# A four-layer hybrid network whose work is woven together by charged costs: other charges for TensorE's products

## The chip, the core and the metric

The kernel runs on one core of a Trainium2 chip. The core has five engines that take their instructions in program order and meet through semaphores: TensorE (PE, matrix products, with PEld for its weight loads), VectorE (DVE), ScalarE (ACT), GpSimd (POOL) and SyncE (SP, which here issues nearly all transfers). The metric is the device time of one execution in microseconds: the median of three runs was 6643.48 us (6634.54 to 6644.86).

## What is computed

An image batch of 4 x 32 x 32 positions with 256 channels runs through four layers. In the reference, cut to what matters here:

```python
# layer 0: selective scan over 1024 positions, 512 channels, 64 states
def step(h, inp):
    xt, dtt, Bt, Ct = inp
    dA = jnp.exp(dtt[:, :, None] * A)
    h = dA * h + (dtt * xt)[:, :, None] * Bt[:, None, :]
    y = jnp.einsum('bdn,bn->bd', h, Ct)
    return (h, y)
...
x = _L0_conv_ref(x, ...)       # norm, product, 3x3 convolution, scan, product
x = _L1_conv_ref(x, ...)       # 1x1, grouped 3x3, 1x1 convolutions
t = t + _L2_attn_ref(_ln_t(t), ...)   # attention of 8 heads over 1024 positions, masked by edges
t = t + _L2_ffn_ref(_ln_t(t), ...)    # 8 experts of 256, best two weighted
t = t + _L3_attn_ref(_ln_t(t), ...)   # products, a scan with 16 states, product
t = t + _L3_ffn_ref(_ln_t(t), ...)    # 8 experts of 512, best two weighted
```

Every expert is computed for every position, and the weights of those not chosen are zero.

## The kernel before

**Two streams of work.** The first is the scans (`scans`, L356). There are eight, one for each of the four images in layer 0 (written (0, b)) and in layer 3 (written (3, b)); `SCANS` (L31) sets their order: (0,0), (0,1), (3,0), (0,2), (3,1), (0,3), (3,2), (3,3). A scan of layer 0 has 256 units of 128 rows x 1024 positions, one of layer 3 has 64, so that there are 1280 units in all. One unit is: a transfer of `dA` (L430), an exponential on ACT (`decay`), two bf16 products on TensorE that spread the inputs into `ps_rep` (`first`, L445), a product and the scan itself on VectorE (`TENSOR_TENSOR` and `TENSOR_TENSOR_SCAN`), and a product on POOL. For every two units, four f32 products with 32 output rows each (`pair`, L460) collect the result in the four quarters of `ps_y`.

The second stream is all other work, in stages (`STAGES`, L33), written as generators. `front` b (norm, convolution and the scan's inputs of layer 0), `middle` b (the end of layer 0, layer 1, attention, the experts of layer 2, and `front3`, which makes the inputs of scan (3, b)) and `last` b (the end of layer 3's scan and its experts). Stage `middle` b can begin when scan (0, b) is done, or, if nothing else can, when its first half is; `last` b likewise after (3, b). `advance` (L530) takes the first stage in the list that can begin and does one step of it.

**How they are woven.** `Metered` (L92) passes each engine call on and adds a charge in microseconds to that engine's clock; the charge of a TensorE product is `matmul_us`. `run` (L552) goes through the scans; twice in every unit it does up to two steps of the current stage, but none as soon as the clock of any engine is ahead of VectorE's:

```python
for e in clock:
    clock[e] = max(clock[e], now - LAG)
for _ in range(TICKS):
    if max(clock.values()) > clock["vector"] + LEAD or self.advance() is None:
        break
```

So the charges fix the order in which instructions stand in each engine's queue, and nothing else. They are worked out when the program is built; they delay nothing at run time.

**When inputs are late.** A scan's inputs are asked for 12 units ahead (`AHEAD`). If the stage that makes them isn't that far, the request is put off until 5 units before they are used (`LATEST`); then `need` (L517) does all steps of the stage that are still missing, one after the other, before the next unit is written. In the text this is a stop of the scans. Inside one, attention (`heads`, L1320) puts its scores into the scan's own PSUM tiles (`ps_sx` in place of `ps_sc`). After the last unit, whatever stages remain are done in a row: the tail.

**Names.** In attention, a key block is one step of `heads`: two score products (`qT`, `kT`, 32 contraction rows), two shifts (`mT`, bf16, 32 rows), two masks (`maskT`, bf16) and four value products with 32 output rows (`ps_at`). In the experts (`moe`, L1442) `ps_h` is the first product (128 x 512 out), `ps_e` the second (128 x 256 out), and `tb` the sum on VectorE. In `front3` (L1624) `ps_p` are the inputs, `ps_g` the gates, `ps_c` the middle product, `ps_x` the small one and `ps_dt` the step sizes. Line 124 of the profile is that of the metered call, and so the line of nearly every instruction.

Of the kernel before, what the change touches and what calls it, by code (L numbers as in the profile page):

```python
# [8 lines left out]
BF16 = mybir.dt.bfloat16  # L9
# [54 lines left out]
def columns(x):  # L64
    n = 1
    for k in x.shape[1:]:
        n *= k
    return n


def matmul_us(out, lhsT=None, rhs=None, **_):
    if lhsT is None:
        lhsT = out
    us = 0.46e-3 * columns(out)
    if lhsT.dtype != BF16:
        us = max(4 * us, 0.3)
    if out.shape[0] <= 32:
        return us / 4
    return us / 2 if lhsT.shape[0] <= 32 else us


def by_columns(per, fixed, of=0):
# [9 lines left out]
class Metered:  # L92


    COST = {
        "tensor": {"matmul": matmul_us, "transpose": lambda out, *_: 0.3},
        "vector": {
            "tensor_tensor": by_columns(1.18, 0.06), "scalar_tensor_tensor": by_columns(1.5, 0.06),
# [1749 lines left out]
```

## Time and profile before

| | us |
|---|---|
| median of 3 runs | 6643.48 |
| the profiled execution | 6636.95 |
| its span, first to last instruction | 6635.2 |
| PE busy | 5360.8 |
| DVE busy | 5224.0 |
| POOL busy | 3653.8 |
| ACT busy, 497 + 96 loads of its table (1.283 each) included | 3439.4 |
| the scans on DVE (1280 of 2.284) | 2924.0 |
| the products before them on DVE (1280 of 1.213) | 1552.8 |

The slices of the page's second part are 165.9 us each. A digit is the busy share in tenths; the row PEclk is the clock granted to TensorE. An f32 product leaves two records in the trace, a bf16 product one, and records of products that overlap are united in a group's busy time, so that its "mean of one" can be much more than its share of the busy time: the 4096 records of `ps_y` in layer 0's scans have a mean of 767 ns and 808.4 us of busy time.

### The profile page before, as it was taken

How to read it: one execution, taken by the hardware profiler on the slowest of the kernel's cores; microseconds unless marked ns; L12 is line 12 of the kernel's file. 1: busy time of each engine (PE TensorE's matmuls, PEld its weight loads, DVE VectorE, ACT ScalarE, POOL GpSimd, SP SyncE). 2: the span in 40 equal slices, each digit the busy share in tenths (PEclk: the TensorE clock that was granted, in tenths of full speed). 3: DMA queues.
4: the chain of work that ended last, by engine and by line, in shares of the span. 5: the costliest groups of instructions: out<-in, count | busy, mean ns of one | idle time of the engine just before them, and what ended most of it. 6: DMA issues, size and time to landing. Idle time of an engine off the chain costs nothing. (4 is left out here: it accounts for less than half of the span.)

```text
span 6635.2 us, 60077 instructions
## 1 busy us (share of the span) xinstructions
PE 5360.8 (81%) x20320; PEld 2159.1 (33%) x20320; DVE 5224.0 (79%) x4489; ACT 3439.4 (52%) x4114; POOL 3653.8 (55%) x1801
## 2 busy tenths in 40 slices
PE   6568778679798577979789779898699679878979
PEld 3003213122253022234235332243245222524656
DVE  8788998988798997789889997798999972248411
ACT  3426666445477334557658544477478344245411
POOL 0876786755557765555766665556856651045200
PEclk8558779589799568979879789989699789887989
DMA  2444554643245566335555664344644750146221
GB/s 74 151 153 157 182 171 163 190 139 124 101 153 170 190 168 155 112 116 172 175 165 168 189 166 133 105 139 169 200 154 161 196 148 21 45 131 169 74 64 35
DMA packets 348112, 936.90 MB, mean 141 GB/s; under 512 B 37140, under 2 KB 119648, under 8 KB 346144
## 3 DMA queue, kind: packets, MB, share of 16 engines
q1 hardware_dynamic: 345616, 930.35, 44.9%
q8 instruction: 172, 2.82, 0.2%
q0 software_dynamic: 2128, 2.13, 0.2%
q14 instruction: 196, 1.61, 0.1%
HBM read 842.59 MB, written 93.95 MB: 141 GB/s over the span
## 5 line engine op out<-in xcount | busy, mean ns | idle before, releaser
L124 POOL TENSOR_TENSOR h<-h,rows 128x1024 f32<-128x1024 f32 x1280 | 3033.0, 2372 | 1900.9 <-DVE h L124 1698.8
L124 DVE TENSOR_TENSOR_SCAN h<-dA,ps_rep 128x1024 f32<-128x1024 f32 x1280 | 2924.0, 2284 | 164.9 <-issue 25.2
L124 DVE TENSOR_TENSOR ps_rep<-ps_rep,rows 128x1024 f32<-128x1024 f32 x1280 | 1552.8, 1213 | 247.7 <-PE ps_rep L124 247.4
L124 ACT ACTIVATE dA<-dA,A_L_conv_A_log 128x1024 f32<-128x1024 f32 x1024 | 1148.6, 1145 | 609.6 <-DMA dA<-dt 528.6
L124 PE MATMUL ps_rep<-S,spread_L_conv_A_log 96*128 96x512 bf16 x2048 | 767.5, 465 | 702.5 <-DVE h L124 674.3
L124 PE MATMUL ps_y<-h,collect_L_conv_A_log 128*32 128x512 f32 x4096 | 808.4, 767 | 77.5 <-POOL h L124 76.5
L124 PE MATMUL ps_h<-xTm,we 128*128 128x512 f32 x1536 | 718.9, 608 | 1.4 <-DVE tb L124 1.4
L124 PE MATMUL ps_e<-we,h_m 128*128 128x256 f32 x3072 | 699.6, 381 | 2.3 <-ACT h_m L124 2.3
L124 ACT ACT_TABLE_LOAD x497 | 637.7, 1283 | 74.7 <-PE ps_h L124 41.7
L124 PEld LDWEIGHTS <-spread_L_conv_A_log 96*128 96x128 bf16 x2048 | 161.4, 103 | 1485.8 <-DVE h L124 1174.6
L124 PEld LDWEIGHTS ps_e<-we,h_m 128*128 128x128 f32 x3072 | 580.8, 190 | 146.8 <-issue 47.2
L124 DVE SCALAR_TENSOR_TENSOR tb<-ps_e,cw,tb 128x256 f32<-128x256 f32 x512 | 220.8, 474 | 411.1 <-PE ps_e L124 410.8
L124 ACT ACTIVATE h_m<-ps_h,cols 128x512 f32<-128x512 f32 x384 | 260.5, 687 | 485.9 <-PE ps_h L124 483.1
L124 ACT ACTIVATE p<-ps_sc 128x512 f32<-128x512 f32 x432 | 234.4, 594 | 474.7 <-PE ps_sc L124 464.8
L124 PEld LDWEIGHTS ps_h<-xTm,we 128*128 128x128 f32 x1536 | 292.9, 194 | 338.5 <-issue 294.0
L124 ACT ACTIVATE dA<-dA,A_L_attn_A_log 128x1024 f32<-128x1024 f32 x256 | 290.2, 1146 | 189.5 <-DMA dA<-dt 166.0
L124 PE MATMUL ps_at<-p,v 128*32 128x512 f32 x1024 | 354.8, 610 | 39.1 <-ACT p L124 28.2
L124 PE MATMUL ps_rep<-S,spread_L_attn_A_log 96*128 96x512 bf16 x512 | 184.9, 449 | 174.2 <-DVE h L124 163.3
L124 PE MATMUL ps_sc<-qT,kT 32*128 32x512 f32 x864 | 251.3, 653 | 30.1 <-issue 30.1
L124 PE MATMUL ps_at<-p,ones 128*32 128x512 f32 x1024 | 271.9, 610 | 0.0
L124 PEld LDWEIGHTS ps_y<-h,collect_L_conv_A_log 128*32 128x32 f32 x4096 | 107.6, 120 | 474.7 <-POOL h L124 226.9
L124 PE MATMUL ps_cv<-pad,diag 128*128 128x512 f32 x576 | 260.4, 594 | 0.0
(313 smaller groups left out, 5027.7 us busy)
## 6 DMA issues: line engine op xcount, KB each, us to landing
dA<-dt SPq DMA_DIRECT2D x1280, 512.0 KB
we<-in_L_ffn_W_dram SPq DMA_DIRECT2D x64, 512.0 KB
parts<-parts SPq DMA_DIRECT2D x64, 384.0 KB
S<-parts SPq DMA_DIRECT2D x96, 256.0 KB
dt<-sp_r SPq DMA_DIRECT2D x64, 256.0 KB
y<-yo SPq DMA_DIRECT2D x128, 128.0 KB
y_back<-y SPq DMA_DIRECT2D x64, 256.0 KB
we<-in_L_ffn_w_dram SPq DMA_DIRECT2D x64, 256.0 KB
```

Of the source, the lines that this page charges most:

```text
L124: return got(*args, **kw)
```

## The change

`matmul_us` gets other charges. No product, no transfer and no wait is added or removed by hand; the order in which the stages' steps stand between the scan units follows from the charges.

```diff
 def matmul_us(out, lhsT=None, rhs=None, **_):
     if lhsT is None:
         lhsT = out
-    us = 0.46e-3 * columns(out)
-    if lhsT.dtype != BF16:
-        us = max(4 * us, 0.3)
-    if out.shape[0] <= 32:
-        return us / 4
-    return us / 2 if lhsT.shape[0] <= 32 else us
+    n = columns(out)
+    few = lhsT.shape[0] <= 32
+    if lhsT.dtype == BF16:
+        return (0.45e-3 if few else 0.72e-3) * n
+    if out.shape[0] <= 32 and n > 32:
+        return 0.86e-3 * n
+    return max(0.09 + (1.1e-3 if few else 1.25e-3) * n, 0.4)
```

| product (output columns) | charge before, us | after |
|---|---|---|
| `ps_rep`, masks: bf16 (512) | 0.236 | 0.369 |
| shifts: bf16, 32 contraction rows (512) | 0.118 | 0.230 |
| `ps_y`, `ps_at`: f32, 32 output rows (512) | 0.236 | 0.440 |
| scores: f32, 32 contraction rows (512) | 0.471 | 0.653 |
| full f32 (512) | 0.942 | 0.730 |
| full f32 (256) | 0.471 | 0.410 |

Transposes keep their charge of 0.3.

## Prediction

> **What bounds the kernel now.** I read the page first, then the busy time by stretch (cut where the stages change), the time line of the scan loop, and the chain of waits.
>
> ```profile
> span 6635.2 us, 60077 instructions
> PE 5360.8 (81%) x20320; PEld 2159.1 (33%) x20320; DVE 5224.0 (79%) x4489; ACT 3439.4 (52%) x4114; POOL 3653.8 (55%) x1801
> ...
> PE   6568778679798577979789779898699679878979
> ...
> DVE  8788998988798997789889997798999972248411
> PEclk8558779589799568979879789989699789887989
> ```
>
> Two loads of about equal size share the span: the scans (VectorE) and everything else (mostly TensorE). Near the end the DVE row drops twice: in slices 34 and 35 (2 2), and from slice 38 on (4 1 1). There TensorE works alone. Everywhere else the scan loop sets the pace:
>
> ```profile
> 299.99 2.29 DVE L124 TENSOR_TENSOR_SCAN h<-dA,ps_rep 128x1024 f32<-128x1024 f32 x1
> 302.20 1.21 DVE L124 TENSOR_TENSOR ps_rep<-ps_rep,rows 128x1024 f32<-128x1024 f32 x1
> 303.53 2.29 DVE L124 TENSOR_TENSOR_SCAN h<-dA,ps_rep 128x1024 f32<-128x1024 f32 x1
> ```
>
> From scan start to scan start an undisturbed unit takes 3.54 to 3.55 us. There are 1280 units; the first scan starts at 204.4, the last at 6194.5. The next rows are stretches: busy time by engine, then granted clock, DMA share and GB/s. They are middle 0, last 0, the stop of the scans at unit 1211, and the tail after the last scan.
>
> ```profile
> 1248.90:2195.90 947.00, 777.76 (x3217) 289.10 (x3217) 806.97 (x660) 518.69 (x634) 558.95 (x268) 0.86 0.43 144
> 3306.20:3739.50 433.30, 387.62 (x1540) 198.03 (x1540) 402.99 (x327) 298.04 (x290) 264.86 (x119) 0.89 0.51 167
> 5494.20:5906.40 412.20, 358.59 (x1391) 165.50 (x1388) 75.76 (x183) 150.87 (x212) 44.58 (x35) 0.92 0.12 38
> 6196.80:6635.20 438.40, 392.77 (x1370) 263.74 (x1368) 60.31 (x154) 79.15 (x119) 17.14 (x13) 0.92 0.14 45
> ```
>
> In the first two the scans run and VectorE is the fuller engine; in the last two VectorE has 76 of 412 and 60 of 438 us. So: **work done beside the scans costs little, work left for a stop or the tail costs its full TensorE time.** I split the 5990.1 us from first to last scan: 1279 steps at 3.55 = 4540; the stop beyond its own step, 412.2 - 3.6 = 409; other VectorE work between the scans, 624 (every such instruction in program order times its group's mean); the remainder, 417, are stalls. By the same split in stretches of 16 units the stalls are 63 in the start and the fronts, 101, 92 and 96 in middles 0 to 2, 8 in each of last 0 and last 1, and 49 after that.
>
> **What the change charges, against what the trace shows.** Per unit the planner charges VectorE 3.55 us, and TensorE two `ps_rep` and two `ps_y` products: 4 x 0.2355 = 0.94 before; 2 x 0.369 + 2 x 0.440 = 1.62 after. What is left for other work is 2.61 before, 1.93 after. In the trace two `ps_rep` take 0.60 and the four `ps_y` of two units 1.06 together, so 1.13 a unit at the most:
>
> ```profile
> 2999.83 0.60 PE L124 MATMUL ps_rep<-S,spread_L_conv_A_log 96*128 96x512 bf16 x2
> ...
> 3000.36 1.06 PE L124 MATMUL ps_y<-h,collect_L_conv_A_log 128*32 128x512 f32 x8
> ```
>
> (x8 is four products: an f32 product leaves two records.) The mean of one `ps_y` record is 767 ns, but four lie beside each other; the new 0.44 charges them 1.76 for 1.06.
>
> One key block of attention (2 scores, 2 shifts, 2 masks, 4 value products) is charged 0.942 + 0.236 + 0.471 + 0.942 = 2.59 before and 1.306 + 0.461 + 0.737 + 1.760 = 4.26 after. In the stop at 5494, without scans, one block follows the other at 2.81 us (5506.79 to 5509.60). Two full products of an expert are charged 1.88 before, 1.46 after, and took 1.72 (four in 3.43, in the chain of work).
>
> So per unit the planner lets in: **attention** 2.61 / 2.59 = 1.0 block before, 1.93 / 4.26 = 0.45 after; a middle has 64 blocks, so 64 units become about 142. **Experts** 2.61 / 1.88 = 1.39 pairs before, 1.93 / 1.46 = 1.32 after: the shorter full products nearly cancel the dearer scan.
>
> The instruction orders of both programs, counted by scan unit (PE's `ps_rep` pairs), show just this. Before to after: front 3 ends at unit 254, 263. Middle 0 ends at 456; after, it isn't ready at 507, where the scan that needs it stops, and ends at 518. Middle 1 ends at 708, 802; last 0 at 814, 915; middle 2 at 1028; after, it isn't ready at 1147 (second stop). Last 1 lies at 1028 to 1134 before; after, it begins at 1222, where last 2 was. Middle 3 begins at 1134, 1158, and both stop at 1211. Behind the last scan lie the end of last 2 and last 3 before, and the end of last 1, last 2 and last 3 after. VectorE's queue is in order: at a stop every later scan step stands behind the stage's own VectorE steps.
>
> **The sum**, against the profiled execution (6636.95 us, span 6635.2).
> - One more last stage in the tail. Last 3 alone runs from the output DMA of last 2 (6328.99) to 6635.2: **+306**. It needs the full TensorE time, and nothing hides it.
> - The stop at 1211 starts with 53 units of middle 3 behind it, not 77: 52 us more attention and other products by these durations, at the rate of the stop: **+53**.
> - The stop at 507: the rest of front3, 8 gate halves, 8 conv, 2 low, 6 dt. In the trace the same run from the first gate product (5817.1) to the next scan (5906.4) takes 89 us; less its own step, **+86**.
> - The stop at 1147: the same with 16 transposes and 8 input halves (14.5 us for the latter in the chain of work, 3.5 for the former at 0.22 each): 107, **+104**.
> - VectorE work that leaves the scan loop: tail 69 to 119 us, stops 83 to 105: **-71**.
> - Stalls, 417 now. Attention proper has 36, 39 and 40 in middles 0 to 2, where TensorE's content is 3.8 to 4.1 us a unit, above the 3.55. After, it is 2.1 to 2.3. The nearest rows are the fronts' convolutions, 3.2 to 3.3 a unit with stalls of 0 per 16 units; I take 1.5 per 16, so 16 a middle: -67. Front3 and last 1 leave the loop: -20. The chains of normalization and routing stay, but lie wider apart: -20. **-107**, with 0 and -417 as ends.
>
> Sum: 306 + 53 + 86 + 104 - 71 - 107 = **+371**. ACT's table loads fall, by the instruction orders, from 597 to 442 (155 x 1.283 = 199 us): worth nothing, ACT is at 52%. With last 1 its loads leave SP's queue and come behind the scans, and at the two new stops the `parts` and `S` transfers and POOL's softplus steps stand ahead of the next scan step: they are inside the 89 us. Between stops ACT waits 694.6 us for `dA` loads and POOL 1698.8 for the scans, both ahead of no one: VectorE's own wait for `ps_rep` is 247.4 in all. Medians stand 6.5 above the profiled execution: 6643.5 + 371 = **7015 us**.
>
> **A rule against it: the clock.** The granted clock is 0.92 in the stop, 0.86 in middle 0, 0.71 in the fronts (TensorE 74% busy). After, attention leaves TensorE emptier. The fronts say that this costs nothing: the clock drops only as far as the load leaves room. The Trainium skill ("TensorE: Matmul & The Clock Gate", part 1) says that an idle window of some 3.4 us puts the array back to half clock. Had attention run at half clock throughout, 2.2 us a unit would take 4.4, and some 480 units would cost 0.85 each: an estimate of 400 us more. No run here shows that yet; the fronts' rows speak against it, and I take the rows.
>
> **Rivals.**
> 1. *Relief is larger* (0.14): stalls fall to about 100, and the two new stops cost only their products (69 + 86, less 7). 371 - 210 - 42 = +119, 6762; this case reaches 6700 to 6870. For it: experts at 3.5 to 3.9 a unit show stalls near 0. Against: the chains between the stages stall at low load too (18 us in the 16 units at 352).
> 2. *No relief* (0.10): stalls stay at 417, now at the restarts. +478, 7122 and up to 7220. For it: after each stop VectorE waits for SP's loads of `S` and `dA`. Against: the units after 1211 show few such stalls.
> 3. *Faster* (0.03): saturation of TensorE during attention was the real price, and thinning it frees more than the tail costs. It decides when the scan step outside stops falls from (5990 - 409) / 1279 = 4.36 us to below 3.93, since 549 us of new stops and tail have to be paid. Its whole store is 417 + 71 = 488; only with the tail and stops at bare products (253 for 306, 148 for 190) does it give 454 - 488 = -34, 6609.
> 4. *Nothing changes* is out: the charges rule the order, and the orders differ from the first fronts on.
>
> **Chances and range.** Forecast 0.73 (6870 to 7110: stalls between 165 and 405), rivals 0.14, 0.10, 0.03. The range 6860 to 7120 leaves out most of rivals 1 to 3. Faster by over 0.2% (13 us, about what a measurement can tell) 0.03, within 0.01, slower 0.96.
>
> **What would show it.** Three long gaps between scan starts, about 89, 107 and 465 us, at units 507, 1147 and 1211, where there is one of 412 now. A tail of some 745 us behind the last scan, with DVE at 1 or 2 tenths. Mean step outside stops about 4.22. PE's clock in attention near 0.7. The busy sums of DVE, PE and POOL unchanged, ACT some 200 less. I am wrong if the step outside stops falls below 4.0, if a stop at 507 costs over 150, or if the tail isn't one last stage longer.

## The result, and the profile after

The changed kernel takes 6921.95 us (median of 4 runs, 6916.13 to 6931.93), the one before 6640.8 beside it: a ratio of 1.0428, 95% interval 1.0414 to 1.0441. It is slower by 281 us; 371 were forecast, and the time lies in the forecast's own range. Of the page of the profile after, the lines that answer to those shown of before:

```profile
span 6914.4 us, 59861 instructions
...
PE 5438.6 (79%) x20320; PEld 2137.0 (31%) x20320; DVE 5221.3 (76%) x4489; ACT 3230.7 (47%) x3943; POOL 3649.0 (53%) x1801
...
PE   6558768778869777787868977886977988697979
...
DVE  8889999989989598998998998998949221861111
PEclk8558769778869888887978987887978889698989
```

The work is the same: as many products, DVE 5221.3 us for 5224.0, POOL 3649.0 for 3653.8; ACT has 209 us less, 199 of them table loads (442 for 597). What changed is where it lies. Up to slice 30 the row DVE is a little fuller than before, but for slices 14 and 30, where the new stops lie; and it ends in four slices with 1 for two. The stretches that answer to the stop and the tail of before (two new stops, the stop at unit 1211, the time behind the last scan):

```profile
2278.80:2359.90 81.10, 73.57 (x173) 29.44 (x171) 9.63 (x11) 39.20 (x58) 23.15 (x18) 0.98 0.19 66
5019.50:5121.80 102.30, 94.69 (x227) 39.36 (x227) 9.65 (x12) 52.25 (x78) 23.17 (x18) 0.96 0.19 62
5406.40:5867.40 461.00, 411.82 (x1668) 178.14 (x1664) 77.91 (x183) 165.47 (x228) 43.21 (x34) 0.92 0.10 30
6164.00:6914.40 750.40, 664.31 (x2310) 448.01 (x2310) 104.84 (x270) 135.21 (x204) 31.94 (x25) 0.91 0.16 48
```

In all four TensorE is 89 to 93% busy and VectorE 9 to 17%. The first one, seen on VectorE's time line:

```profile
2278.81 2.29 DVE L125 TENSOR_TENSOR_SCAN h<-dA,ps_rep 128x1024 f32<-128x1024 f32 x1 
2332.95 0.69 DVE L125 SCALAR_TENSOR_TENSOR sp_e<-ps_dt,sp_e 128x512 f32<-128x512 f32 x1 [51.85 <-ACT sp_l L125]
...
2358.68 1.22 DVE L125 TENSOR_TENSOR ps_rep<-ps_rep,rows 128x1024 f32<-128x1024 f32 x1 
2359.93 2.29 DVE L125 TENSOR_TENSOR_SCAN h<-dA,ps_rep 128x1024 f32<-128x1024 f32 x1 
```

The next scan step isn't slow, it stands behind front3's own steps (`sp_e`, `sp_x`), and these wait, through ACT, for front3's products:

```profile
2328.45 0.69 ACT L125 ACTIVATE sp_r<-ps_dt,cols 128x512 f32<-128x512 f32 x1 [2.95 <-PE ps_dt L125]
```

So 81 us pass from one scan start to the next. Against this, the scan loop between the stops got faster. Attention of middle 0, from its first to its last value product, before and after:

```profile
1465.70:1741.60 275.90, 264.58 (x1380) 70.06 (x1380) 213.79 (x135) 141.75 (x209) 145.66 (x65) 0.98 0.35 116
```

```profile
1487.60:1978.00 490.40, 399.59 (x1823) 84.82 (x1824) 462.31 (x283) 221.92 (x285) 317.85 (x139) 0.83 0.46 146
```

Before, 57 scan steps start in 275.9 us (4.84 us each), TensorE is 96% busy and VectorE 77%. After, 131 start in 490.4 us (3.74 each), TensorE is 81% busy and VectorE 94%. VectorE's wait for `ps_rep` fell from 247.4 us to 98.2 over the whole run:

```profile
DVE ps_rep L125 <- PE ps_rep L125: 98.2, 69, 8.4
```

The sum, by the split of the prediction, made alike for every kernel (steps of 3.55 us; scan gaps over 30 us are stops; products behind the last scan are the tail). Counted this way the kernel before has 413 us of stalls and 628 of other VectorE work. Stalls are the remainder, so an error in the other work shows in them with the opposite sign; these two columns are good to some 13 us.

| kernel | stops | tail | other VectorE work | stalls | span |
|---|---|---|---|---|---|
| before | 412 | 441 | 628 | 413 | 6635 |
| after | 81 + 102 + 461 | 753 | 557 | 228 | 6914 |

Stops +232 (each new one less its own step: +225), tail +312, VectorE work -71, stalls -185, first scan 2 earlier: +279, the difference of the spans.

### The profile page after: what moved, and what is told of

It reads as the page before. It is cut to its first block, busy times and chain, and to the rows that moved or that the text cites. A ratio compares the mean times of both kernels' runs of the same rounds, so it can differ in the third digit from the quotient of the medians.

```text
span 6914.4 us, 59861 instructions
## 1 busy us (share of the span) xinstructions
PE 5438.6 (79%) x20320; PEld 2137.0 (31%) x20320; DVE 5221.3 (76%) x4489; ACT 3230.7 (47%) x3943; POOL 3649.0 (53%) x1801
## 5 line engine op out<-in xcount | busy, mean ns | idle before, releaser
L125 DVE TENSOR_TENSOR ps_rep<-ps_rep,rows 128x1024 f32<-128x1024 f32 x1280 | 1549.7, 1211 | 98.7 <-PE ps_rep L125 98.2
L125 PE MATMUL ps_y<-h,collect_L_conv_A_log 128*32 128x512 f32 x4096 | 786.3, 761 | 79.0 <-POOL h L125 79.0
L125 ACT ACTIVATE p<-ps_sc 128x512 f32<-128x512 f32 x400 | 217.1, 594 | 778.9 <-PE ps_sc L125 778.8
L125 PE MATMUL ps_at<-p,v 128*32 128x512 f32 x1024 | 340.5, 704 | 12.2 <-ACT p L125 11.6
L125 PE MATMUL ps_at<-p,ones 128*32 128x512 f32 x1024 | 317.4, 703 | 0.0
L125 PE MATMUL ps_sc<-qT,kT 32*128 32x512 f32 x800 | 274.6, 761 | 29.9 <-issue 22.6
L125 POOL TENSOR_TENSOR sp_l<-sp_l,sp_e 128x512 f32<-128x512 f32 x64 | 81.0, 1266 | 387.2 <-DVE sp_e L125 351.6
```

The source lines that it names most:

```text
L125: return got(*args, **kw)
```

## The experiments

Each kernel was timed in three rounds beside the kernel before. The prediction's account is theory A; B says that each charge costs in proportion; C says that the dearer attention made the stages late, which is where the prediction laid the weight. Where a cut of `matmul_us` below has a minus line, it gives the old charge in the changed function's form. The split of all runs stands behind the last one.

**One charge at a time.** e1: only the narrow f32 products, the change's line `return 0.86e-3 * n`, all else as before.

```diff
     if out.shape[0] <= 32 and n > 32:
-        return 0.46e-3 * n
+        return 0.86e-3 * n
```

> Only the f32 products with 32 output rows get the new charge (0.44), all others the old one. Theory A (time = scan steps at 3.55 us + other VectorE work between them + stalls of a TensorE that is over-full in attention + work in stops and tail at TensorE's rate): by the instruction order middle 3 now begins when the last stop comes, so the stop at unit 1211 holds 590 us of products for 333 (+252), a small new stop at 507 (+30), tail +21, VectorE work out of the loop -66, stalls -170: about 6708 us (6660 to 6750). Theory B (time follows the total charge, each part in proportion; the whole change charges about 823 us more and cost 281): +733 charged, so +250: about 6890. A also expects one gap of about 660 us between scan starts at unit 1211 and a tail of about 460.

Measured: 6694.6 us, ratio 1.008 (1.0061 to 1.01). The total is A's and not B's, but by two misses of A that nearly cancel: the stop at 1211 takes 726 us for some 660, and the stalls fall by 243 for 170. The stop at 507 takes 34.

e2: only the other f32 products.

```diff
-    return max((0.92e-3 if few else 1.84e-3) * n, 0.3)
+    return max(0.09 + (1.1e-3 if few else 1.25e-3) * n, 0.4)
```

> Only the charges of the other f32 products change (full 0.73 for 0.94, scores 0.65 for 0.47), narrow and bf16 ones keep the old charge. Theory A: attention thins a little (0.885 key blocks a unit, 3.5 to 3.7 us of TensorE a unit), experts thicken to 4.3 to 4.8; stop at 1211 as before, tail -27, stalls -30 to -50: about 6575 us (6530 to 6640). Theory B: 377 us less charged, so -128: about 6513. A third theory, that the shorter full products are what cost the time because the experts over-fill TensorE, expects more than 6700.

Measured: 6788.65 us, ratio 1.0222 (1.0204 to 1.024). A missed by 214 us and B by more; the third theory is right. Stop (413) and tail (421) came about as said, but the stalls rose from 413 to 586. Counted per 16 units they show where. TensorE's content below is a unit's products at the rates of the stops and the tail of before, as an estimate: 0.86 us for a full f32 product of 512 columns, 0.43 for one of 256, 2.81 for a key block, and 0.86 for the scan's own as e11 charges them. In the 16-unit stretches of last 0 where most experts lie, the content is 4.1 to 4.3 us a unit in place of 3.5, with 3 to 7 us of stalls in place of none; the two last stages in the loop have 50 each for 8. The fronts (units 64 to 255), with up to 4.1 for 3.3, go from about 50 to about 100. Last 0's stretch in this kernel:

```profile
3338.30:3748.20 409.90, 371.54 (x1442) 197.56 (x1438) 350.56 (x292) 254.69 (x254) 224.87 (x102) 0.87 0.46 154
```

It has 89 units in 410 us, 4.6 us each; before it had 106 in 433, 4.1 each, with VectorE at 93% and not at 86%. Against the scans, last 0 is over sooner, and then, in 32 units before middle 2 may begin, no other work is there at all. In last 0's stretch VectorE waits 26.1 us for `ps_rep` and 12.5 for `ps_e`, 6.7 and 1.8 before. **Bunching is the harm:** the same work, taken faster than VectorE can hide it, and then nothing to hide.

e3: the changed kernel with the narrow products back at 0.46e-3 (the opposite of e1's edit).

> The changed kernel with the narrow f32 products back at their old charge (0.236). Theory A: no new stops, the stop at 1211 +17, the tail one last stage as before (-12), attention at 2.8 to 3.0 us a unit, so its stalls go (-115) and some others (-25): about 6515 us (6480 to 6560), faster than both kernels. Theory B: about 90 us more charged than before, so about 6671, slower than before. The fully opposite case: if the relief doesn't come from attention, 6640 to 6660.

Measured: 6628.57 us, ratio 0.9986 (0.9976 to 0.9996). Neither. Stop (433) and tail (432) are A's and attention's stalls are gone (2.8 to 3.0 us of TensorE a unit, 0 to 5 us per 16 units), but the fronts and experts took them back, as in e2: 395 in all.

e4: one charge of attention raised, all else as before.

```diff
-    return max((0.92e-3 if few else 1.84e-3) * n, 0.3)
+    return max((1.5e-3 if few else 1.84e-3) * n, 0.3)
```

> The kernel before with one charge raised: scores 1.5e-3 a column for 0.92e-3 (0.768 for 0.471 us), so that attention alone goes slower (0.82 blocks a unit for 1.0, 3.3 to 3.5 us of TensorE a unit); fronts and last stages stay as they were, tail the same, stop at 1211 +14. Theory A: the stalls of attention proper (115 in middles 0 to 2) go for the most part: -80, about 6560 us (6530 to 6590). Theory B: 152 us more charged, +52: about 6693. If the relief came from thinner experts or fewer table loads: 6640 to 6660.

Measured: **6502.82 us, ratio 0.9801 (0.978 to 0.9822)**, the fastest of all. It lies below A's range: A's sign and mechanism hold, but the relief is twice what A gave it (stalls 413 to 254). B is out. Fewer table loads aren't the reason, there are 588 for 597. The changed line also reaches 32 products of `ps_dt` in the fronts and 64 of `ps_b` in the experts, some 19 us of charge beside the 152 of the scores. The same stretch of attention as above:

```profile
1464.70:1751.40 286.70, 276.45 (x1463) 72.78 (x1464) 260.89 (x164) 156.86 (x223) 178.32 (x79) 0.98 0.41 139
```

Against before it lasts 11 us longer and carries 72 scan steps for 57. TensorE is 96% busy, as before, and VectorE 91%: both are full. VectorE's wait for `ps_rep`:

```profile
DVE ps_rep L125 <- PE ps_rep L125: 123.6, 97, 7.8
```

**Scan or attention?** e5 gives the new charges to the scan's own products alone: `ps_rep` 0.369 in `matmul_us`, and beside each `ps_y` product

```diff
                     start=(i == 0), stop=(i == per - 1), tile_position=(0, at),
                 )
+                self.clock["tensor"] += 0.205
```

> The kernel before, with the new charges for the scan's own products alone (ps_rep 0.369, ps_y 0.440); attention, experts and fronts keep the old ones. Theory A (stops and tail at TensorE's rate, set by how much room the dearer scan leaves): by the instruction order a new stop at 507 with 52 us of products and a tail with last 1, last 2 and last 3, 648 us of products, as in the changed kernel; gaps of about 64 and 458, tail about 770, stalls down to about 180: 6775 us (6720 to 6830). Theory C (the dearer attention is what makes the stages late): about the time before, 6600 to 6680, with one last stage in the tail.

Measured: 6805.16 us, ratio 1.0242 (1.0225 to 1.0259). A holds, C doesn't. Stops 66 and 460, and last 1 to last 3 stand behind the last scan:

```profile
6036.60:6807.40 770.80, 684.52 (x2376) 459.35 (x2368) 108.84 (x275) 139.32 (x210) 32.41 (x26) 0.91 0.15 47
```

e6 gives the new charges to attention alone (0.205 more beside each `ps_at` product; 0.72e-3 and 0.45e-3 for bf16 products other than `ps_rep`; 0.65 for a score).

> The kernel before, with the new charges for attention's products alone (values 0.440, masks 0.369, shifts 0.230, scores 0.65): 0.61 key blocks a unit for 1.0. Theory A: the attention stalls go, stalls about 225; no new stop, the stop at 1211 holds 449 us of products for 333 (a gap of about 540), tail unchanged at 441: about 6560 us (6520 to 6600), faster than before. Theory C: slower than before, 6750 or more.

Measured: 6598.28 us, ratio 0.9939 (0.9922 to 0.9955). A holds (by 2 us at the edge), C doesn't. Attention takes 97 units in place of 57, no new stop appears, the tail stays and stalls are 248. Something does come late: the first product of middle 3 stands at unit 1209 for 1159, and the stop at 1211 takes 551, 139 more; the relief of 165 pays for it.

e7: only the bf16 charges.

```diff
     if lhsT.dtype == BF16:
-        return (0.23e-3 if few else 0.46e-3) * n
+        return (0.45e-3 if few else 0.72e-3) * n
```

> The kernel before with the new bf16 charges alone (ps_rep and masks 0.369, shifts 0.230). Theory A: everything a little thinner (3.0 to 3.5 us of TensorE a unit), stalls about 190; the stop at 1211 holds 447 us (gap about 540), tail about 449, no other stop: about 6530 us (6490 to 6590). Theory B (cost in proportion to the charge): 467 us more charged, +159: about 6797.

Measured: 6581.11 us, ratio 0.9905 (0.9888 to 0.9921). A, with the stalls 45 us higher than said. B is out.

e9: the changed kernel with the scan's own products at the old charges (0.46e-3 for `ps_rep`, 0.205 taken off beside `ps_y`).

> The changed kernel with only the scan's own products back at their old charges (ps_rep and ps_y 0.236); attention stays dear (0.61 key blocks a unit), full products stay short. Theory A: no new stops, the stop at 1211 with 352 us of products (gap about 436), the tail 357 us (about 421); fronts and layer 3's experts over-full as in e2_full (4.0 to 4.9 us of TensorE a unit), attention thin: stalls about 505, so about 6730 us (6690 to 6770). Theory C (the dearer attention makes the stages late): close to the changed kernel, 6850 to 6920.

Measured: 6732.77 us, ratio 1.0145 (1.0128 to 1.0162). A: stop 431, tail 418, stalls 499. C is out a third time: attention at the new charge brings no new stop and no longer tail as long as the scan's own products stay cheap (and the full ones short).

**Filling the last scan.** e8 starts from e4 and lets two steps a turn through whatever the clocks say, from turn 2432 on. With two turns a unit that is unit 1216, where the last scan begins, five units behind the stop.

```diff
                 for _ in range(TICKS):
-                    if max(clock.values()) > clock["vector"] + LEAD or self.advance() is None:
+                    lead = LEAD if n < 2432 else 1e6
+                    if max(clock.values()) > clock["vector"] + lead or self.advance() is None:
```

> The kernel of e4_scores, and from unit 1211 on the planner no longer stops at VectorE's clock (two steps at every turn), so that last 2 is done whole beside the last scan. Theory A: TensorE is over-full there, which costs nothing as the work would else stand in the tail: products behind the last scan 245 us for 379, tail about 300, the last 67 units about 330 us: about 6400 us (6380 to 6460). If an over-full TensorE beside a scan always costs what it costs in e2_full, no gain: 6480 to 6520.

Measured: 6533.56 us, ratio 0.9835 (0.9819 to 0.9851), 31 us slower than e4. Both cases missed: it is slower than either range. The tail is 293, as said, but from the stop's end to the last scan step it takes 465 us where e4 has 286. Two stretches of it, units 1232 to 1247 and 1264 to 1279:

```profile
5907.20:6056.60 149.40, 148.95 (x526) 87.82 (x527) 70.76 (x70) 78.44 (x83) 36.46 (x16) 0.94 0.36 97
6189.60:6245.80 56.20, 32.42 (x97) 3.87 (x94) 51.11 (x30) 18.08 (x17) 42.09 (x20) 0.57 0.74 178
```

First TensorE is full and VectorE half empty, then last 2 is over and the rest of the scan runs bare: bunching again. In the first of the two, VectorE waits 72 of 149 us for the experts' products, whose sums (`tb`) stand in its queue ahead of the next scan steps:

```profile
DVE tb L125 <- PE ps_e L125: 71.6, 16, 10.0
```

e10 takes one step a turn:

```diff
-                for _ in range(TICKS):
-                    lead = LEAD if n < 2432 else 1e6
+                late = n >= 2432
+                for _ in range(1 if late else TICKS):
+                    lead = 1e6 if late else LEAD
```

> e8_scores_late with one step a turn in place of two from unit 1211 on, so that last 2 is spread over all units of the last scan and none of them stays without other work. Theory A: about 4 us of TensorE a unit there, 352 us of products behind the last scan for 379: tail about 418, the last units about as in e4_scores: 6485 us (6460 to 6510). If filling beyond 3.9 us a unit costs as much as it saves: 6500 to 6530.

Measured: 6519.68 us, ratio 0.9817 (0.9801 to 0.9833): the second case. The tail gave 31 us back, and the stalls took 48.

**Charges by the rates of a full TensorE.** e11 takes 0.86 us for a full f32 product of 512 columns and scales the others from it (the lines added):

```diff
+    if lhsT.dtype == BF16:
+        return (0.21e-3 if few else 0.42e-3) * n
+    if out.shape[0] <= 32 and n > 32:
+        return 0.42e-3 * n
+    return max((0.84e-3 if few else 1.68e-3) * n, 0.3)
```

> Charges that follow what a product really takes of TensorE when it is full, read off the stop at 5494 and the tail of the kernel before: full 0.860, scores 0.43, ps_rep and masks 0.215, shifts 0.11, the products with 32 output rows 0.215 (four beside each other). The planner then fills TensorE to about 3.55 us a unit everywhere, in clumps up to 4.4. Theory A with the corrected threshold (a stall where TensorE's content is over 3.55 plus the unit's other VectorE work): stop at 1211 with 321 us of products (gap about 400), tail about 425, stalls about 500 as attention, fronts and layer 3's experts are all over-full: about 6700 us (6640 to 6790), slower than before. If true charges are the best charges: below 6600.

Measured: 6822.77 us, ratio 1.0274 (1.0256 to 1.0291). Slower than before, as A said, but 120 us above its figure and outside its range: stalls are 615, and attention at 4.2 us a unit stalls 16 to 20 us per 16 units. But these charges are not true everywhere. They give a key block 2.37 us, which takes 2.81 in the stop (5506.79 to 5509.60), and so they let in 1.1 blocks a unit. What charges that are true for attention too would do, no run shows. VectorE's wait:

```profile
DVE ps_rep L125 <- PE ps_rep L125: 396.8, 251, 8.3
```

All runs, in us, by the same split:

| kernel | stops | tail | other VectorE work | stalls | span | ratio |
|---|---|---|---|---|---|---|
| before | 412 | 441 | 628 | 413 | 6635 | 1 |
| after | 644 | 753 | 557 | 228 | 6914 | 1.0428 |
| e1 narrow | 760 | 459 | 562 | 170 | 6692 | 1.008 |
| e2 other f32 | 413 | 421 | 631 | 586 | 6790 | 1.0222 |
| e3 narrow undone | 433 | 432 | 626 | 395 | 6626 | 0.9986 |
| e4 scores | 436 | 442 | 625 | 254 | 6496 | 0.9801 |
| e5 scan dear | 526 | 771 | 564 | 209 | 6807 | 1.0242 |
| e6 attention dear | 551 | 441 | 611 | 248 | 6592 | 0.9939 |
| e7 bf16 | 547 | 452 | 610 | 235 | 6584 | 0.9905 |
| e8 late, two steps | 434 | 293 | 645 | 423 | 6539 | 0.9835 |
| e9 scan undone | 431 | 418 | 628 | 499 | 6714 | 1.0145 |
| e10 late, one step | 436 | 411 | 630 | 302 | 6520 | 0.9817 |
| e11 rates | 411 | 428 | 630 | 615 | 6828 | 1.0274 |

Two columns pull against each other. Dearer charges thin the loop: stalls fall from 413 to some 170 to 250, but stops and tail grow. Cheaper ones bunch it: stalls rise to 500 and 600, and stops and tail hardly shrink. In e2 and e11 the first products of middles 2 and 3 stand at units 839 and 1159, as before, right behind the scans (0,2) and (0,3) that end at 832 and 1152, however early the work ahead of them is over. The parts don't add up: 0.8, -0.95 and 2.2% alone, 4.3 together.

## Why the prediction was right, and where it wasn't

*What bounds the kernel, and the tail.* Right. One more last stage lies in the tail, which grew by 312 for 306: last 3 runs from the output transfer of last 2 (6608.8) to the end, 306 us as before, last 2 takes 301 ahead of it (from 6308.1), and the rest of the stage before them takes 12 more. e5 makes the same tail with the scan's charges alone.

*The stops.* Right in place and nearly in size: 81 us for 89 at unit 507, 102 for 107 at 1147, 461 for 465 at 1211; over their own steps and the old stop, +78, +99 and +49 for 86, 104 and 53.

*VectorE work that leaves the loop.* -71, as forecast.

*Stalls.* This is the term that was mis-sized: -185 for -107, 78 of the 90 us between forecast and result. The mean step outside the stops is 4.16 us for the 4.22 forecast. Attention proper was given 1.5 us per 16 units and mostly has 0 to 0.5, so that it gives 111 and not 67; the end of the middles and last 1 give some 36 for 20; the chains of normalization and routing and the beginnings of stages give some 38 for 20. e4 confirms the mechanism by itself: with attention alone thinned, stalls fall by 159 and VectorE's wait for `ps_rep` halves. The forecast looked only at 3.55 us a unit as the bound of TensorE's content. Stretches of experts and of convolutions fit a bound of 3.55 plus the unit's other VectorE work. For this the scan's own products are taken at 1.03 us a unit, from start to start in the prediction's rows (0.53 for two `ps_rep`, 0.99 for the four `ps_y` of two units, up to the next product below), which puts 0.17 on the contents above. The forecast's own contents (2.1 to 2.3 for attention) come out with 0.86, not with the 1.13 that it works out.

```profile
3001.35 0.48 PE L124 MATMUL ps_e<-we,h_m 128*128 128x256 f32 x1
```

Layer 2's experts then stand at 4.36 us a unit in e4 (units 640 to 655 and 960 to 975), with 13.3 us of other work in 16 units just under their bound of 4.38, and stall 0.2 to 0.4 us. The fronts' convolutions in e2 (from units 80, 128 and 192 on), with no other VectorE work, stand at 4.04, 4.26 and 4.31 and stall 7.9, 10.5 and 11.5 us per 16 units, where the bound gives 7.8, 11.3 and 12.1. Attention doesn't fit: 17 key blocks in 16 units stall 9 to 11 us before, 15 stall 6 to 8 in e2 and 19 stall 19 in e11, where the bound gives 4, none and 10. So what attention stalls beyond its mean content stays open.

*"The shorter full products nearly cancel the dearer scan"* and *attention as what fills the loop.* The first is right in the changed kernel (experts at 3.3 to 3.9 us a unit, stalls near 0) but hides that each half harms by itself, and e2 shows the one, e5 the other. The second put the weight on the wrong charge. Middle 0's attention does go from 57 units to 131, but e6 and e9 show that the dearer attention without the dearer scan brings no new stop and no longer tail, and by itself it gains (e6). The scan's own products, charged 1.62 us a unit in place of 0.94, take 0.68 us of room from every stage in every unit, and e5 shows what that does alone: the stop at 507 (66 us) and the whole extra tail. The stop at 1147 (102 us) stands in the changed kernel only, so it takes the scan's charges and others together.

*The clock.* That a lower clock costs nothing came true, its size didn't: in attention the granted clock was 0.83, not near 0.7, and stalls were mostly 0 to 0.5 us per 16 units. PE's busy sum grew by 78 us, which the forecast had unchanged. Half clock does exist in this kernel, in bare stretches, where nothing but the scans runs: 0.53 between 2160 and 2397 before, and there the products take nearly twice as long (1.04 us for 0.60 and 1.94 for 1.06 in the prediction's rows):

```profile
2300.41 1.04 PE L124 MATMUL ps_rep<-S,spread_L_conv_A_log 96*128 96x512 bf16 x2 [2.50 <-DVE h L124]
2301.38 1.94 PE L124 MATMUL ps_y<-h,collect_L_conv_A_log 128*32 128x512 f32 x8
```

The rule of the Trainium skill ("TensorE: Matmul & The Clock Gate", part 1), by which an idle window of some 3.4 us halves the clock, doesn't fit these rows as it stands: only 3 of the 62 idle stretches of TensorE there are longer than 3.4 us, the usual ones last 2.5 us or less. The 400 us that were worked out from it are not there; in woven attention the mean clock stays at 0.83.

*The rivals.* The relief was larger, as the first had it, but a third of the way only; the restarts after the three stops stall by 4 us each, in the two units behind them, so the second fell; the third would have needed 549 us of relief and got 256 (stalls and VectorE work together).

## What to carry to other kernels

When one stream is woven under another, price it by where it ends up: beside the engine that bounds the loop, and as long as the stretch isn't over-full, it costs little more than its own work on that engine, behind it the full time. A planner's charges are levers: a charge 63% higher for one product of an over-full stage was faster by 2.0%, while charges by the rates of full products, which under-charge attention, were slower than the old ones by 2.7%. Before a charge is corrected, count which stretches of the loop are over-full and which are empty, and move only the former; a charge that every unit pays, like the scan's own, takes room from all stages at once.

## What the runs showed of the hardware

Four f32 products with 32 output rows each, in the four quarters of one PSUM tile, took 1.06 us together, while one of their records has a mean of 767 ns. Eight such products that all go to the same 32 rows took 6.98 us, 0.87 each:

```profile
5858.26 6.98 PE ps_x L124 x16
```

So the four beside each other were 3.3 times as fast as one behind the other. The Trainium skill gives 2.38 times for three products packed by columns ("TensorE: Matmul & The Clock Gate", part 3, measured speedup). The changed charge of 0.44 fits neither: a product's share is 0.27 at the most where four lie beside each other, and 0.87 where they don't.

Unexpected was how far both engines fill at once: in e4's attention TensorE is 96% and VectorE 91% busy over 287 us, with the granted clock at 0.98.
